# An expert's w1 and v1 products rewritten as seven block products of 64 tokens, two at a time in column halves

## Chip, core and metric

The kernel runs on one core of one Trainium2 chip. The metric is the device time of a launch in microseconds. In the profile PE is TensorE's matmuls, PEld its weight loads, DVE is VectorE, ACT is ScalarE, POOL is GpSimd and SP is the queue that issues most transfers.

## What is computed

Everything is float32. An input of 4 x 1024 tokens with 1024 channels is layer-normed (`xn`), and the result is the sum of three parts:

```
x + attention(xn) + moe(xn)
attention: q = xn Wq, v = xn Wv, a decaying scan of v over the tokens, y = q * state,
           layer norm of y, y * silu(xn Wg), then y Wo
moe:       softmax over 64 experts, the top 8 of each token, at most C = 128 tokens per expert
           h = silu(xg w1') * (xg v1')     xg: 128 tokens x 1024, w1 and v1: 384 x 1024
           out[token] += weight * (h w2)   w2: 384 x 1024
```

The change touches the line `h = ...` for each of the 64 experts.

## The kernel before

**Stages.** The first half of the span, up to about 1225 us, computes v, q and gate for four batch rows. Each 1024 x 1024 product of that half, and the output projection Wo, is already done as a two by two block product with seven instead of eight block products (`steps`, `left_sums`, `right_sums`; the matmuls are line 137). Weight blocks with their sums (tile `w`, seven slots) are read through a pool with two buffers (`pools.left`), one load per product on the SP queue. After that comes the expert stage: a loop over 64 experts, into which 16 units of the output projection (`project`, seven steps of four float32 matmuls each) are spread, so that most experts carry two such steps, some one or three, and the last three none.

**One expert before.** `fetch(e + 2)` loads w1 and v1 two experts ahead and gathers the tokens' rows by an indirect transfer on POOL (line 849). `turned` transposes the gathered rows on DVE (867). `hidden` runs 8 matmuls of 128 tokens x 384 columns for w1 and 8 for v1 (line 884) into two PSUM banks; between the two, PE transposes the hidden values of the expert before (903), which DVE copies to `hT` (904). `gate` is a Silu on ACT (894) and a product on DVE (895). `output` runs six matmuls for w2 (914), scales the rows on DVE (917), and POOL adds them to the output in DRAM (925). A float32 matmul is two records in the profile: 16 matmuls are x32.

**Buffers.** Weights go through five buffers in rotation (`pools.x`, two, and `pools.y`, three), so that three loads per expert can run ahead. PSUM banks come by tag: a, b and c have two buffers each, r and t one.

**Order.** From the fourth expert on, the order on each engine is the scheduler's; only the first three experts are pinned on DVE and PE (`in_order`). A bank or a tile is released by the last instruction that reads it, and a writer waits for that.

Of the kernel before, what the change touches and what calls it, by code (L numbers as in the profile page):

```python
# [8 lines left out]
F32 = mybir.dt.float32  # L9
I32 = mybir.dt.int32  # L10
AF = mybir.ActivationFunctionType
ALU = mybir.AluOpType
# [4 lines left out]
P = 128  # L17
B, S, D = 4, 1024, 1024
NTOK = B * S
KD = D // P  # L20
KH = KD // 2
SH = S // 2
NM = SH // P
E, K, F, C = 64, 8, 384, 128
KF = F // P
Q = 32
NQ = P // Q
DQ = D // NQ
# [12 lines left out]
NSLOT = 7  # L41
# [2 lines left out]
BLOCKS = ((0, 0), (1, 0), (1, 1), (0, 1))  # L44

H0, H1 = slice(0, SH), slice(SH, S)


def left_sums(eng, t, pin=lambda ins: None):

    pin(eng.tensor_tensor(t[:, 4], t[:, 3], t[:, 2], ALU.add))
    eng.tensor_tensor(t[:, 5], t[:, 4], t[:, 0], ALU.subtract)
    eng.tensor_tensor(t[:, 3], t[:, 0], t[:, 3], ALU.subtract)
    eng.tensor_tensor(t[:, 6], t[:, 1], t[:, 5], ALU.subtract)
# [23 lines left out]
@contextmanager  # L78
def in_order(tc, engines=None):

    traced = tc.nc.cur_bb.bb.instructions
    begin = len(traced)
    yield
    last = {}
    for ins in list(traced[begin:]):
        if engines is not None and ins.engine not in engines:
            continue
        if ins.engine in last:
            tc.add_manual_dep(
                ins,  # L90
                last[ins.engine].name,
                mybir.DependencyInfo(mybir.DependencyClass.NoSync, mybir.DependencyReason.DATA),
                reason="in order",
            )
        last[ins.engine] = ins
# [137 lines left out]
def attn_and_routing(  # L233
# [193 lines left out]
    def load_turned(b, h):  # L427
# [5 lines left out]
        for r0, xs, _, _ in stored[b, h]:  # L433
            for j in range(2):
                from_ = rows[r0 + j * P : r0 + (j + 1) * P, :]
                for q in range(NQ):
                    loaded = nc.sync.dma_start(
                        out=xs[q * Q : (q + 1) * Q, j + 1, :].rearrange("i (r c) -> i r c", r=NQ),
                        in_=from_[:, q * DQ : (q + 1) * DQ].rearrange("(r i) c -> i r c", i=Q),
                    )  # L440
# [378 lines left out]
class Experts:  # L819


    def __init__(self, tc, pools, ident, rows, wtab, gated, wo, w1, v1, w2, out):
        self.tc, self.nc, self.pools, self.ident = tc, tc.nc, pools, ident
        self.rows, self.wtab, self.gated = rows, wtab, gated
        self.wo, self.ws, self.out = wo, ((w1, KD), (v1, KD), (w2, KF)), out
        self.weights, self.tokens, self.wo_b, self.loaded = {}, {}, {}, 0

    def load(self, e, n):


        if e >= E:
            return
        pools, (w, k) = self.pools, self.ws[n]
        t = (pools.x if self.loaded % 5 < 2 else pools.y)(f"w{n}_{e}")
        self.loaded += 1
        t = t.rearrange("p a b -> p (a b)")
        self.nc.sync.dma_start(out=t, in_=w[e])
        self.weights[e, n] = t.rearrange("p (k f) -> p k f", k=k)

    def fetch(self, e):  # L840

        if e >= E:
            return
        nc, pools = self.nc, self.pools
        for n in range(2):
            self.load(e, n)
        xg = pools.quarter.tile([P, NQ, DQ], F32, tag="quarter", name=f"xg_{e}")
        for r in range(NQ):
            nc.gpsimd.indirect_dma_start(  # L849
                out=xg[:, r, :],  # L850
                out_offset=None,
                in_=self.rows.rearrange("n (q c) -> (n q) c", q=NQ),
                in_offset=bass.IndirectOffsetOnAxis(ap=self.part[:, r, e : e + 1], axis=0),
            )
        wt = pools.small.tile([P, E], F32, tag="wt", name=f"wt_{e}")
        nc.gpsimd.indirect_dma_start(  # L856
            out=wt,
            out_offset=None,
            in_=self.wtab,
            in_offset=bass.IndirectOffsetOnAxis(ap=self.idx[:, e : e + 1], axis=0),  # L860
        )
        self.tokens[e] = xg, wt[:, e : e + 1]

    def turned(self, e):

        xT = self.pools.line.tile([P, KD, P], F32, tag="line", name=f"xgT_{e}")
        done = self.nc.vector.transpose(  # L867
            xT.rearrange("p k (r i) -> p k r i", i=Q),
            self.tokens[e][0].rearrange("p r (k j) -> p k r j", j=Q),
        )  # L870
        if e == 0:
            self.tc.keep_in_program_order(done)
        return xT

    def hidden(self, e, xT, before):


        pools = self.pools
        ph, hT = [], None
        for n in range(2):  # L880
            ps = pools.bank("ab"[n], [P, F], f"h{n}_{e}")
            w = self.weights.pop((e, n))
            for k in range(KD):
                self.nc.tensor.matmul(  # L884
                    ps, lhsT=xT[:, k, :], rhs=w[:, k, :], start=(k == 0), stop=(k == KD - 1)
                )
            ph.append(ps)
            if n == 0 and before is not None:
                hT = self.turned_hidden(*before)
        return ph, hT  # L890

    def gate(self, e, ph):
        act = self.pools.one.tile([P, F], F32, tag="cur", name=f"act_{e}")
        self.nc.scalar.activation(act, ph[0], AF.Silu)
        self.nc.vector.tensor_tensor(act, act, ph[1], ALU.mult)  # L895
        return act

    def turned_hidden(self, e, act):
        nc, pools = self.nc, self.pools
        hT = pools.line.tile([P, KF, P], F32, tag="line", name=f"hT_{e}")  # L900
        pt = pools.bank("t", [P, KF, P], f"hpt_{e}")
        for j in range(KF):
            nc.tensor.transpose(pt[:, j, :], act[:, j * P : (j + 1) * P], self.ident)  # L903
        nc.vector.tensor_copy(hT, pt)  # L904
        return e, hT

    def output(self, e, hT):
        nc, pools = self.nc, self.pools
        w2, wt = self.weights.pop((e, 2)), self.tokens.pop(e)[1]
        ys = pools.line.tile([P, D], F32, tag="line", name=f"ys_{e}")  # L910
        for h, cols in enumerate((H0, H1)):
            ps = pools.bank("cr"[h], [P, SH], f"y_{e}_{h}")
            for j in range(KF):
                nc.tensor.matmul(  # L914
                    ps, lhsT=hT[:, j, :], rhs=w2[:, j, cols], start=(j == 0), stop=(j == KF - 1)
                )
            nc.vector.tensor_scalar(ys[:, cols], ps, wt, None, ALU.mult)  # L917
            if e == E - 1:
                halves = self.out.rearrange("n (h c) -> (n h) c", h=2)
                self.add(halves, self.ends[:, h : h + 1], ys[:, cols])  # L920
        if e < E - 1:
            self.add(self.out, self.idx[:, e : e + 1], ys)
# [35 lines left out]

    def begin(self, idx, part, ends):
        self.idx, self.part, self.ends = idx, part, ends  # L960
        self.fetch(0)

    def turn_first(self):
        self.turn = self.turned(0)

    def run(self):
        nc, units = self.nc, B * NM
        gated = self.load_gated(0)
        self.fetch(1)
        self.load_wo()  # L970
        self.load(0, 2)


        begins = [1 + u * (E - 4) // units for u in range(units)] + [E - 3]
        before, todo, u, many = None, None, 0, iter(())
        for e in range(E):

            kept = [mybir.EngineType.DVE, mybir.EngineType.PE] if e < 3 else []
            with in_order(self.tc, kept):
                ph, turned_before = self.hidden(e, self.turn, before)  # L980
                self.fetch(e + 2)
                self.load(e + 1, 2)
                if e == 0:
                    self.turn = self.turned(e + 1)
                act = self.gate(e, ph)
                if 0 < e < E - 1:
                    self.turn = self.turned(e + 1)
                if e == 0:
                    right_sums(nc.vector, self.wo_b, lambda n: self.pools.block(f"wo_{n}"))
                if before is not None:  # L990
                    self.output(*turned_before)
                before = e, act
                if u < units and e == begins[u]:
                    todo = self.project(u, gated)
                    many = iter((3, 2, 2) if begins[u + 1] - e == 3 else (2, 2, 2, 1))
                    u += 1
                    gated = self.load_gated(u) if u < units else None
                for _ in range(next(many, 0)):
                    next(todo, None)
        self.output(*self.turned_hidden(*before))  # L1000


# [46 lines left out]
```

## Time and profile before

| | |
|---|---|
| median of 3 runs | 2642.36 us (2641.43 to 2643.7) |
| the profiled execution's own time | 2641.28 us |
| its span | 2639.3 us |
| granted TensorE clock, mean | 0.998 |
| PE busy | 2617.9 us, 99% of the span |
| DVE, ACT, POOL busy | 1108.6, 315.6, 696.5 us |
| DMA in the expert stage (1600 to 2500 us) | 0.86 to 0.91 busy, 274 to 296 GB/s |

Busy times overlap across engines. A group of the profile names the line, the engine, the output and input tiles, the shape and the number of records, then busy time and the mean duration of one. Matmul durations overlap each other[...]; their pace is read from the chain of waits (a start, a length, a count), not from the mean.

### The profile page before, as it was taken

The page shows a single profiled execution, that of the slowest core. Times are in us where ns is not written, and L with a number is a line of the kernel's source. Part 1 is how long each engine was busy: PE and PEld are TensorE (multiplying, and loading weights), DVE is VectorE, ACT ScalarE, POOL GpSimd, SP SyncE. Part 2 cuts the span into 40 slices and gives each one's busy share as a digit, 9 for nine tenths or more (in the row PEclk, how much of TensorE's full clock was granted, in tenths as well). Part 3 has the DMA queues.
Part 4 walks back from the last instruction along what each step waited for, and adds up shares of the span by engine and source line. Part 5 has one row for each costly group of instructions (what it writes and reads, how often), then busy time and mean ns, then how long its engine had stood idle before and what let it go on. Part 6 is the DMA issues. An engine that isn't in the chain of part 4 may idle for free.

```text
span 2639.3 us, 18523 instructions
## 1 busy us (share of the span) xinstructions
PE 2617.9 (99%) x6917; PEld 1269.6 (48%) x6917; DVE 1108.6 (42%) x1414; ACT 315.6 (12%) x472; POOL 696.5 (26%) x631
## 2 busy tenths in 40 slices
PE   9999999999999999999999999999999999999997
PEld 5444444444444444444555555555555555555554
DVE  8946686465935686273222222222222221222221
ACT  4113111131112211121000000000000000000000
POOL 1452312111030102122323323333333333333231
PEclk9999999999999999999999999999999999999999
DMA  5665434442444522328889988899889988999886
GB/s 188 247 199 203 171 127 139 176 171 92 148 131 167 203 84 84 147 97 329 263 269 304 295 287 277 282 296 290 285 280 289 302 280 280 287 288 302 265 282 178
DMA packets 122474, 592.95 MB, mean 225 GB/s; under 512 B 15872, under 2 KB 52736, under 8 KB 89360
## 3 DMA queue, kind: packets, MB, share of 16 engines
q1 hardware_dynamic: 81488, 448.03, 47.4%
q0 software_dynamic: 40464, 143.72, 20.1%
q8 instruction: 55, 0.90, 0.1%
q14 instruction: 35, 0.29, 0.0%
q10 hardware_dynamic: 432, 0.01, 0.0%
HBM read 483.67 MB, written 124.81 MB: 231 GB/s over the span
## 4 chain that ended last, share of the span: by engine, by line
PE 95%; DVE 4%; issue 0%; DMA 0%; POOLq 0%; ACT 0%; DVEq 0%
PE h L884 25%; PE y L914 12%; PE pa_g L137 8%; PE pa_o L137 8%; PE pa_q L137 7%; PE pa_v L137 7%; PE pc_g L137 4%; PE pc_o L137 4%; PE pc_v L137 4%; PE pc_q L137 4%; PE pb_o L137 2%; PE pb_g L137 2%; PE pb_q L137 2%; PE pb_v L137 2%; PE lg L475 1%; DVE cur L548 1%
## 5 line engine op out<-in xcount | busy, mean ns | idle before, releaser
L884 PE MATMUL h<-w,xgT 128*128 128x384 f32 x2048 | 682.1, 486 | 0.0
L884 PEld LDWEIGHTS h<-w,xgT 128*128 128x128 f32 x2048 | 384.5, 190 | 268.9 <-issue 32.5
L849 POOL DMA_INDIRECT xg<-rows,tables x256 | 250.9, 980 | 404.4 <-DVE xgT L867 333.0
L914 PE MATMUL y<-w,hT 128*128 128x512 f32 x768 | 340.1, 592 | 1.0 <-DVE hT L904 1.0
L137 PE MATMUL pa_g<-xT,w 128*128 128x512 f32 x512 | 230.7, 593 | 0.0
L914 PEld LDWEIGHTS y<-w,hT 128*128 128x128 f32 x768 | 145.9, 190 | 170.9 <-issue 153.0
L904 DVE COPY hT<-hpt 128x384 f32<-128x384 f32 x64 | 35.7, 558 | 438.1 <-PE hpt L903 433.4
L137 PE MATMUL pa_q<-xT,w 128*128 128x512 f32 x480 | 216.6, 593 | 3.0 <-DVE y L172 3.0
L137 PE MATMUL pa_v<-xT,w 128*128 128x512 f32 x480 | 215.9, 592 | 0.0
L917 DVE TENSOR_SCALAR ys<-y,wt 128x512 f32<-128x512 f32 x128 | 96.0, 750 | 239.3 <-PE y L914 239.3
L137 PE MATMUL pa_o<-wo_T,gated 128*128 128x512 f32 x384 | 172.6, 592 | 0.0
L137 PEld LDWEIGHTS pa_g<-xT,w 128*128 128x128 f32 x512 | 96.9, 190 | 122.3 <-issue 121.7
L137 PEld LDWEIGHTS pa_v<-xT,w 128*128 128x128 f32 x480 | 91.2, 190 | 114.9 <-issue 109.9
L137 PEld LDWEIGHTS pa_q<-xT,w 128*128 128x128 f32 x480 | 90.5, 190 | 115.9 <-issue 109.7
L925 POOL DMA_INDIRECT out_dram<-ys,tables x63 | 102.2, 1623 | 153.4 <-DMA out_dram<-ohi 105.0
L856 POOL DMA_INDIRECT wt<-wtab,tables x64 | 62.3, 973 | 288.9 <-DVE ys L917 250.5
L684 POOL DMA_DIRECT2D gated<-y x64 | 48.5, 763 | 323.5 <-DVE y L679 312.6
L895 DVE TENSOR_TENSOR act<-act,h 128x384 f32<-128x384 f32 x64 | 35.5, 554 | 229.6 <-PE h L884 229.6
L137 PEld LDWEIGHTS pa_o<-wo_T,gated 128*128 128x128 f32 x384 | 73.0, 190 | 90.9 <-issue 89.9
L137 PE MATMUL pc_g<-xT,w 128*128 128x512 f32 x256 | 115.7, 592 | 0.0
L137 PE MATMUL pc_q<-xT,w 128*128 128x512 f32 x256 | 115.5, 593 | 0.0
L137 PE MATMUL pc_v<-xT,w 128*128 128x512 f32 x256 | 115.4, 593 | 0.0
(210 smaller groups left out, 2474.7 us busy)
## 6 DMA issues: line engine op xcount, KB each, us to landing
w<-in_w_dram SPq DMA_DIRECT2D x128, 1536.0 KB, 7.7
w<-in_v_dram SPq DMA_DIRECT2D x64, 1536.0 KB, 9.7
w<-wsum SPq DMA_DIRECT2D x36, 1792.0 KB, 7.7
wsum<-w POOLq DMA_DIRECT2D x12, 1792.0 KB, 6.1
x<-in_x_dram SPq DMA_DIRECT2D x32, 512.0 KB, 9.2
rows<-x POOLq DMA_DIRECT2D x32, 512.0 KB, 7.4
gated<-y POOLq DMA_DIRECT2D x64, 256.0 KB, 3.3
gated<-gated SPq DMA_DIRECT2D x16, 1024.0 KB, 10.4
```

The lines of the kernel that those rows point to most:

```text
L137: nc.tensor.matmul(ps, lhsT=lhs[:, slot, k, :], rhs=blocks[right][:, k, :], start=start and k == 0, stop=stop and k == KH - 1, skip_group_ ...
L475: nc.tensor.matmul(two[h * E : (h + 1) * E, :], lhsT=r_sb[:, k, :], rhs=blocks[f"B{k // KH + 1}{h + 1}"][:, k % KH, :], start=(k == KD - 1 ...
L548: nc.vector.match_replace(cur, eight, cur, 0.0)
L684: nc.gpsimd.dma_start(out=gated[b, :, :, slot, m, :].rearrange("u p j -> p u j"), in_=yc[:, h * SH : (h + 1) * SH].rearrange("p (u j) -> p ...
L849: nc.gpsimd.indirect_dma_start(out=xg[:, r, :], out_offset=None, in_=self.rows.rearrange("n (q c) -> (n q) c", q=NQ), in_offset=bass.Indir ...
L856: nc.gpsimd.indirect_dma_start(out=wt, out_offset=None, in_=self.wtab, in_offset=bass.IndirectOffsetOnAxis(ap=self.idx[:, e : e + 1], axis=0),
L884: self.nc.tensor.matmul(ps, lhsT=xT[:, k, :], rhs=w[:, k, :], start=(k == 0), stop=(k == KD - 1))
L895: self.nc.vector.tensor_tensor(act, act, ph[1], ALU.mult)
L904: nc.vector.tensor_copy(hT, pt)
L914: nc.tensor.matmul(ps, lhsT=hT[:, j, :], rhs=w2[:, j, cols], start=(j == 0), stop=(j == KF - 1))
L917: nc.vector.tensor_scalar(ys[:, cols], ps, wt, None, ALU.mult)
L925: self.nc.gpsimd.indirect_dma_start(out=to, out_offset=bass.IndirectOffsetOnAxis(ap=rows, axis=0), in_=ys, in_offset=None, compute_op=ALU.add,
```

## The change

The two products of an expert are treated as one product of a two by two block matrix (tokens in halves of 64, channels in halves of 512) with another one (channels in halves of 512, the two blocks of columns being w1 and v1). It takes seven block products of 64 x 512 x 384 instead of eight. A block product has only 64 stationary columns, so two different ones are issued alternately, one to the left and one to the right half of the array's columns (`tile_position`), and land in partitions 0 to 63 and 64 to 127 of a PSUM bank.

DVE forms four sums of the weights (T1 to T4, 128 x 1536 each) and four of the tokens (128 x 256 each) per expert. ACT moves some halves of banks across partitions, DVE adds the products up, and the scaling of the output rows goes from DVE to ACT. PE, DVE and ACT are held in program order through the whole expert stage. w1 and v1 get two fixed buffers each, w2 a single one. One of the two buffers of `pools.left` is now kept for T2 and T3 (`places`), and the first unit of the projection begins with the first expert.

```diff
+ORDERED = [mybir.EngineType.PE, mybir.EngineType.DVE, mybir.EngineType.Activation]
 def load(self, e, n):
-        t = (pools.x if self.loaded % 5 < 2 else pools.y)(f"w{n}_{e}")
+        slot = (n, e % 2) if n < 2 else n
+        if slot not in self.slots:
+            t = (pools.x if e == 0 and n < 2 else pools.y)(f"w{n}_{e}")
+            self.slots[slot] = t.rearrange("p a b -> p (a b)")
+        t = self.slots[slot]
+def places(self):
+        t = pools.left.tile([P, NSLOT, KH, P], F32, tag="w", name="t23")
+        u = pools.block("t4").rearrange("p a b -> p (a b)")
...
+def left_sums(self, e):
+        a11, a12, a21, a22 = self.left_blocks(e)
+        vector.tensor_tensor(s3, a11, a21, ALU.subtract)
+        vector.tensor_tensor(s1, a21, a22, ALU.add)
+        vector.tensor_tensor(s2, s1, a11, ALU.subtract)
+        vector.tensor_tensor(s4, a12, s2, ALU.subtract)
+def sums31(self, e):
+            b11, _, b12, b22 = self.right_blocks(e)
+            self.nc.vector.tensor_tensor(self.t3, b22, b12, ALU.subtract)
+            self.nc.vector.tensor_tensor(b12, b12, b11, ALU.subtract)
+def sums24(self, e):
+            _, b21, t1, b22 = self.right_blocks(e)
+            self.nc.vector.tensor_tensor(self.t2, b22, t1, ALU.subtract)
+            self.nc.vector.tensor_tensor(self.t4, b21, self.t2, ALU.subtract)
 def hidden(self, e):
-        for n in range(2):
-            for k in range(KD):
-                self.nc.tensor.matmul(
-                    ps, lhsT=xT[:, k, :], rhs=w[:, k, :], start=(k == 0), stop=(k == KD - 1)
+        ba, bb, bc, bd = (pools.bank(tag, [P, F], f"h{tag}_{e}") for tag in "abcr")
+        def both(left, right):
+            for k in range(len(left[3])):
+                for half, (bank, a, b, ks) in ((lo, left), (hi, right)):
+                    nc.tensor.matmul(bank[half], lhsT=a[:, ks[k], :], rhs=b[:, ks[k], :],
+                        start=(k == 0), stop=(k == len(ks) - 1), tile_position=(0, half.start))
+        both((bc, s3, self.t3, every), (bc, s4, b22, every))
+        self.sums31(e + 1)
+        both((ba, a11, b11, every), (bb, s1, t1, every))
+        nc.scalar.copy(act[lo], ba[lo])
+        nc.scalar.copy(act[hi], ba[lo])
+        nc.scalar.copy(up[lo], bb[hi])
+        nc.vector.tensor_tensor(mid, bc, act, ALU.add)
+        both((bb, s2, self.t2, every), (bd, a12, b21, every))
+        nc.scalar.copy(up[hi], bb[lo])
+        nc.vector.tensor_tensor(up, mid, up, ALU.add)
+        nc.vector.tensor_tensor(up, bb, up, ALU.add)
+        nc.vector.tensor_tensor(mid[lo], bb[lo], mid[lo], ALU.add)
+        both((bd, a22, self.t4, (0, 1)), (ba, a22, self.t4, (2, 3)))
+        nc.scalar.copy(act[lo], ba[hi])
+        nc.vector.tensor_tensor(act, bd, act, ALU.add)
+        nc.vector.tensor_tensor(act[lo], act[lo], mid[lo], ALU.add)
+        nc.scalar.activation(act, act, AF.Silu)
+        self.turned(e + 1)
+        nc.vector.tensor_tensor(act, act, up, ALU.mult)
+        self.left_sums(e + 1)
+        self.sums24(e + 1)
 def output(self, e):
-            ps = pools.bank("cr"[h], [P, SH], f"y_{e}_{h}")
+            ps = pools.bank("br"[h], [P, SH], f"y_{e}_{h}")
-            nc.vector.tensor_scalar(ys[:, cols], ps, wt, None, ALU.mult)
+            nc.scalar.mul(ys[:, cols], ps, wt)
 def run(self):
-        begins = [1 + u * (E - 4) // units for u in range(units)] + [E - 3]
+        begins = [u and 1 + u * (E - 4) // units for u in range(units)] + [E - 3]
+        with in_order(self.tc, ORDERED):
+            self.sums24(0)
+            for e in range(E):
+                if e > 0:
+                    self.turn_hidden(e - 1)
+                self.hidden(e)
+                self.fetch(e + 2)
+                if e == 0:
+                    right_sums(nc.vector, self.wo_b, lambda n: self.pools.block(f"wo_{n}"))
+                else:
+                    self.output(e - 1)
+                    self.load(e, 2)
...
+            self.turn_hidden(E - 1)
+            self.output(E - 1)
```

The four calls of `both` are called the first to the fourth quarter below; the first three have four pairs of matmuls each, the fourth has two.

More of the change, by code (lines that the diff above doesn't have):

```diff
@@ L25 @@
 KF = F // P
+TH = P // 2
 Q = 32
@@ L825, in __init__ @@
         self.wo, self.ws, self.out = wo, ((w1, KD), (v1, KD), (w2, KF)), out
-        self.weights, self.tokens, self.wo_b, self.loaded = {}, {}, {}, 0
+        self.weights, self.xTs, self.wo_b, self.slots, self.xg = {}, {}, {}, {}, None
     def load(self, e, n):
@@ L833, in load @@
         pools, (w, k) = self.pools, self.ws[n]
-        t = (pools.x if self.loaded % 5 < 2 else pools.y)(f"w{n}_{e}")
-        self.loaded += 1
-        t = t.rearrange("p a b -> p (a b)")
+        slot = (n, e % 2) if n < 2 else n
[3 more added lines that the diff above has]
+        t = self.slots[slot]
         self.nc.sync.dma_start(out=t, in_=w[e])
@@ L844, in fetch @@
         nc, pools = self.nc, self.pools
-        for n in range(2):
+        for n in (1, 0):
             self.load(e, n)
-        xg = pools.quarter.tile([P, NQ, DQ], F32, tag="quarter", name=f"xg_{e}")
+        if self.xg is None:
+            self.xg = pools.block("xg").rearrange("p k (x c) -> p (k x) c", c=DQ)
         for r in range(NQ):
             nc.gpsimd.indirect_dma_start(
-                out=xg[:, r, :],
+                out=self.xg[:, e % 2 * NQ + r, :],
                 out_offset=None,
@@ L854, in fetch @@
             )
-        wt = pools.small.tile([P, E], F32, tag="wt", name=f"wt_{e}")
         nc.gpsimd.indirect_dma_start(
-            out=wt,
+            out=self.wt[:, e % NQ, :],
             out_offset=None,
@@ L861, in fetch @@
         )
-        self.tokens[e] = xg, wt[:, e : e + 1]
+    def places(self):
+        pools = self.pools
+        t = pools.left.tile([P, NSLOT, KH, P], F32, tag="w", name="t23")
+        t = t.rearrange("p a b c -> p (a b c)")
+        u = pools.block("t4").rearrange("p a b -> p (a b)")
+        n = KH * F
+        self.t2, self.t3, self.t4 = (
+            v.rearrange("p (k f) -> p k f", f=F) for v in (t[:, 0:n], t[:, n : 2 * n], u[:, 0:n])
+        )
+        self.up, self.mid = t[:, 2 * n : 2 * n + F], u[:, n : n + F]
+        self.s = pools.one.tile([P, 4, KH, TH], F32, tag="cur", name="s")
     def turned(self, e):
+        if e >= E:
+            return
         xT = self.pools.line.tile([P, KD, P], F32, tag="line", name=f"xgT_{e}")
@@ L868, in turned @@
             xT.rearrange("p k (r i) -> p k r i", i=Q),
-            self.tokens[e][0].rearrange("p r (k j) -> p k r j", j=Q),
+            self.xg[:, e % 2 * NQ : (e % 2 + 1) * NQ].rearrange("p r (k j) -> p k r j", j=Q),
         )
@@ L872, in turned @@
             self.tc.keep_in_program_order(done)
[L873 to L879, printed above, removed]
-        for n in range(2):
-            ps = pools.bank("ab"[n], [P, F], f"h{n}_{e}")
-            w = self.weights.pop((e, n))
-            for k in range(KD):
-                self.nc.tensor.matmul(
-                    ps, lhsT=xT[:, k, :], rhs=w[:, k, :], start=(k == 0), stop=(k == KD - 1)
[L886 to L898, printed above, removed]
-        nc, pools = self.nc, self.pools
[L900 to L905, printed above, removed]
@@ L907, in output @@
-    def output(self, e, hT):
-        nc, pools = self.nc, self.pools
-        w2, wt = self.weights.pop((e, 2)), self.tokens.pop(e)[1]
+        self.xTs[e] = xT
+    def left_sums(self, e):
+        if e >= E:
+            return
+        vector = self.nc.vector
+        a11, a12, a21, a22 = self.left_blocks(e)
+        s1, s2, s3, s4 = (self.s[:, i] for i in range(4))
+        vector.tensor_tensor(s3, a11, a21, ALU.subtract)
+        vector.tensor_tensor(s1, a21, a22, ALU.add)
+        vector.tensor_tensor(s2, s1, a11, ALU.subtract)
+        vector.tensor_tensor(s4, a12, s2, ALU.subtract)
@@ new lines, in left_blocks, with right_blocks @@
+    def left_blocks(self, e):
+        xT = self.xTs[e]
+        return [xT[:, k : k + KH, i : i + TH] for i in (TH, 0) for k in (0, KH)]
+    def right_blocks(self, e):
+        return [self.weights[e, n][:, k : k + KH] for n in range(2) for k in (0, KH)]
+    def sums31(self, e):
+        if e < E:
+            b11, _, b12, b22 = self.right_blocks(e)
+            self.nc.vector.tensor_tensor(self.t3, b22, b12, ALU.subtract)
+            self.nc.vector.tensor_tensor(b12, b12, b11, ALU.subtract)
@@ new lines, in sums24, with hidden @@
+    def sums24(self, e):
+        if e < E:
+            _, b21, t1, b22 = self.right_blocks(e)
+            self.nc.vector.tensor_tensor(self.t2, b22, t1, ALU.subtract)
+            self.nc.vector.tensor_tensor(self.t4, b21, self.t2, ALU.subtract)
+    def hidden(self, e):
+        nc, pools = self.nc, self.pools
+        a11, a12, _, a22 = self.left_blocks(e)
+        b11, b21, t1, b22 = self.right_blocks(e)
+        s1, s2, s3, s4 = (self.s[:, i] for i in range(4))
+        ba, bb, bc, bd = (pools.bank(tag, [P, F], f"h{tag}_{e}") for tag in "abcr")
+        lo, hi = slice(0, TH), slice(TH, P)
+        def both(left, right):
+            for k in range(len(left[3])):
+                for half, (bank, a, b, ks) in ((lo, left), (hi, right)):
+                    nc.tensor.matmul(
+                        bank[half],
+                        lhsT=a[:, ks[k], :],
+                        rhs=b[:, ks[k], :],
+                        start=(k == 0),
+                        stop=(k == len(ks) - 1),
+                        tile_position=(0, half.start),
+                    )
+        every, act, up, mid = range(KH), self.act, self.up, self.mid
+        both((bc, s3, self.t3, every), (bc, s4, b22, every))
[19 more added lines that the diff above has]
+        self.sums24(e + 1)
+        for n in range(2):
+            del self.weights[e, n]
@@ L910, in output, with turn_hidden @@
+    def turn_hidden(self, e):
+        nc, pt = self.nc, self.pools.bank("t", [P, KF, P], f"hpt_{e}")
+        for j in range(KF):
+            nc.tensor.transpose(pt[:, j, :], self.act[:, j * P : (j + 1) * P], self.ident)
+        nc.scalar.copy(self.hT, pt)
+    def output(self, e):
+        nc, pools = self.nc, self.pools
+        w2, wt, hT = self.weights.pop((e, 2)), self.wt[:, e % NQ, e : e + 1], self.hT
         ys = pools.line.tile([P, D], F32, tag="line", name=f"ys_{e}")
         for h, cols in enumerate((H0, H1)):
-            ps = pools.bank("cr"[h], [P, SH], f"y_{e}_{h}")
+            ps = pools.bank("br"[h], [P, SH], f"y_{e}_{h}")
@@ L960, in begin @@
         self.idx, self.part, self.ends = idx, part, ends
+        v = self.pools.line.tile([P, S], F32, tag="line", name="act")
+        self.act, self.hT = v[:, 0:F], v[:, F : 2 * F].rearrange("p (j i) -> p j i", i=P)
+        self.wt = v[:, 2 * F :].rearrange("p (x e) -> p x e", e=E)
         self.fetch(0)
     def turn_first(self):
-        self.turn = self.turned(0)
+        self.places()
+        self.turned(0)
+        self.left_sums(0)
+        self.sums31(0)
     def run(self):
         nc, units = self.nc, B * NM
-        gated = self.load_gated(0)
         self.fetch(1)
         self.load_wo()
+        gated = self.load_gated(0)
         self.load(0, 2)
-        begins = [1 + u * (E - 4) // units for u in range(units)] + [E - 3]
[L975 to L980, printed above, removed]
-                self.fetch(e + 2)
[L982 to L987, printed above, removed]
+        begins = [u and 1 + u * (E - 4) // units for u in range(units)] + [E - 3]
+        todo, u, many = None, 0, iter(())
+        with in_order(self.tc, ORDERED):
[4 more added lines that the diff above has]
+                self.hidden(e)
+                self.fetch(e + 2)
                 if e == 0:
                     right_sums(nc.vector, self.wo_b, lambda n: self.pools.block(f"wo_{n}"))
-                if before is not None:
-                    self.output(*turned_before)
-                before = e, act
+                else:
+                    self.output(e - 1)
+                    self.load(e, 2)
                 if u < units and e == begins[u]:
@@ L996, in run @@
                     u += 1
-                    gated = self.load_gated(u) if u < units else None
                 for _ in range(next(many, 0)):
                     next(todo, None)
-        self.output(*self.turned_hidden(*before))
+                if u < units and e + 1 == begins[u]:
+                    gated = self.load_gated(u)
+            self.turn_hidden(E - 1)
+            self.output(E - 1)
 def kernel(**inputs):
```

## The prediction

> **What bounds the kernel now.** First the page's busy times and its clock row: PE is busy 99% of the span at full clock. Then the costliest groups and the chain that ended last, in order of time:
>
> ```profile
> PE 2617.9 (99%) x6917; PEld 1269.6 (48%) x6917; DVE 1108.6 (42%) x1414; ACT 315.6 (12%) x472; POOL 696.5 (26%) x631
> ...
> PEclk9999999999999999999999999999999999999999
> ```
> ```profile
> 2004.97 5.16 PE h L884 x16
> 2010.13 5.15 PE y L914 x12
> ```
> ```profile
> 908.85 7.09 PE lg L475 x32
> 915.94 1.05 PE pa_g L137 x2
> ...
> 917.43 2.58 PE pc_g L137 x6
> ```
>
> So a stage is worth what it takes from PE, and any wait put into PE's order counts in full. The pace of a record is length over count: 5.16/16 = 0.3225 us for 384 columns, 2.58/6 = 0.430 for 512. An expert's `h` is 32 records, 10.32 us; with the three transposes (0.33) and `y` (5.15) it is 15.8 us, plus 3.43 per step of the output projection.
>
> The rows of the router's logits (L475) are the near relation of the change: 64 stationary columns, the two halves of the array in turn, each with its own moving data. 32 records take 7.09 us, 0.222 each, half of 0.430. The halves run at the same time.
>
> **The change, part by part.**
>
> *Matmuls.* Fourteen pairs of float32 matmuls, 28 pairs of records, replace 32 records: 28 x 0.3225 = 9.03 us, 1.29 less per expert. Here a rule speaks against the change. The Trainium skill, "TensorE: Matmul & The Clock Gate", Part 3, says a weight load overlaps a running matmul only where the two use different rows of the array; both halves use all rows. By the rule each pair would add a load (137 ns in the L475 weight-load group) and cost 0.46, 12.9 us in all, 3.8 more than by the row. The row decides: pairs of 512 ran at the undivided matmul's pace. At 384 columns there is less time for the two loads, but 2 x 137 = 274 ns still lies under 322.
>
> *Switch to halves and back.* The logits' stretch: 7.09 - 16 x 0.430 = 0.21, and the next two whole records take 1.05 instead of 0.86, 0.19 more. I add 0.40 per expert (0.3 to 0.5).
>
> *A wait inside each expert.* In the built program's order the first matmul of the third quarter waits for ScalarE's copy of `bb[hi]` to `up[lo]`, in all 64 experts: that quarter writes the other half of the same bank. In ScalarE's order, now fixed, two other copies stand before it, and all three need the second quarter's end. Nothing follows on PE meanwhile, as the order is fixed. ScalarE's nearest rows:
>
> ```profile
> L894 ACT ACTIVATE act<-h 128x384 f32<-128x384 f32 x64 | 31.4, 490 | 593.5 <-PE hpt L903 590.2 <-PE h L884 3.3
> L299 ACT COPY xT<-pt 128x512 f32<-128x512 f32 x16 | 8.6, 587 | 6.3 <-PE pt L298 6.1
> ```
>
> 384 elements out of PSUM take 490 ns. Sixteen copies of 587 are 8.6 us busy instead of 9.4, in pairs, so neighbours overlap by 0.1: three take 0.39 + 0.39 + 0.49 = 1.27. In the timeline of before `y`'s first record starts at 2009.96 and DVE's L895, which waits for the last of `h`, at 2010.23: a reader starts 0.25 or so after PE has gone on. In the other direction the last `y` follows its `hT` by 0.05 (DVE's copy ends at 2620.30, PE starts at 2620.35). 0.25 + 1.27 + 0.05: 1.57 us of idle PE per expert; ends 1.27 (no latency) and 1.85 (no overlap).
>
> Per expert: -1.29 + 0.40 + 1.57 = +0.68; x 64 = **+43.5 us**. The gain of the seventh-of-eight product is smaller than the wait that serves it.
>
> *A second wait, 13 times.* In the expert after a unit of the projection has begun, `pb_o` still holds a b bank, since DVE adds it up only behind the next weight sums. `y`'s first half then waits for DVE's last read of `hb`: from the third quarter's end 0.25 + copy 0.49 + DVE 0.05 + 0.59 + 0.48 + 0.55 = 2.4, against a fourth quarter of 1.29 and 0.1 of switch: 1.0 each, **+13**. Three units of three experts have their last two steps next to each other, with a DVE sum between: **+3**.
>
> *At the start of the stage: the last gate product.* T2 and T3 take one of the two weight buffers before the last gate product's weights are loaded. Its load now waits for the end of the product before, and PE waits for the load. Two rows, a lone w1 load and a load of this kind:
>
> ```profile
> w<-in_w_dram SPq DMA_DIRECT2D x1, 1536.0 KB, 6.2
> ```
> ```profile
> w<-wsum SPq DMA_DIRECT2D x1, 1792.0 KB, 8.0
> ```
>
> 6.2 x 1792/1536 = 7.2 from issue, 0.6 of latencies, and 0.9 as the last step now follows its DVE read directly: 8.7 (8 to 10). PE is idle for 7.7 of it. The Trainium skill, same page, Part 1, says the clock falls to half after an idle window of about 3.4 us. No run of before has such an idle in its middle, but its start shows the price:
>
> ```profile
> 2.08 7.81 PE L246 MATMUL warm<-zero,ident 128*128 128x512 f32 x12 [2.08 <-DVE best L273]
> ```
>
> Twelve records of 0.43 would be 5.15, and the last one's tail 0.16: 2.5 lost. By the row alone a gap in the middle could cost nothing; by the rule each gap over 3.4 costs 2.5, while 1.57 costs none. I take the rule: **+11.2**.
>
> *Expert 1.* Behind the weight sums for expert 1, DVE has the four sums of Wo (4 x 2.32 from L64's 2291 ns) and four of the projection's left block (2.6). By a clock from the start of `hidden(0)`: quarters end at 2.8 and 5.4, after the wait at 9.5 and 10.8. DVE's `mid[lo]` ends 2.4 after the third, at 11.9; two more adds (554 ns each) bring 13.0, the transpose (1234) 14.2, the product 14.7, four token sums 16.3, T2 and T4 19.8. Then 9.3 for Wo and 2.6: 31.8; then 3.5 of sums for expert 2, which in program order come before expert 1's own `mid`; four combinations later, near 37.5, `mid[lo]` is done. PE had two projection steps (6.9), the transposes (0.3) and `hidden(1)` (10.9) behind 10.9, so at 29.0 it needs the bank: 8.5 idle, 7.5 beyond the 1.0 counted, and the clock 2.5: **+10** (5 to 12).
>
> *The end.* w2 has one buffer. Expert 63's load is issued after `y` of 62 and needed at once: 6.2 to 8.3, say 6.7, + 0.3, less the 1.5 that PE waits for `hT` there anyway: 5.5, and the clock 2.5: **+8** (5 to 10).
>
> *At nothing.* DVE's four weight sums are 1.76 each (2291 x 1536/2048, + 40 ns), the token sums 1.7, with the combinations, the transpose and a share of the projection 15 us per expert of some 22.5; on the clock of expert 0 above, s3 and s4 are ready at 16.3, and PE asks for them at 16.4 even without a projection step (10.9 + 5.15 + 0.33), at 20 to 23 with one or two. If DVE were later by x in each expert, x would come on top, 64-fold. The next expert's weights are now needed at 3 us into `hidden`, some 20 us earlier than before; their loads are issued from 5.4 and 9.5 us on in the expert before, so 14 to 20 us remain for a landing of 7.7 to 9.8 (page, part 6). Scaling on ScalarE (0.6 twice) leaves it under 6 us busy per expert. POOL's list is the same; its index transfers overlap DVE's two-input sums in before without either growing (683 ns with and without).
>
> Sum: 43.5 + 13 + 3 + 11.2 + 10 + 8 = 88.7 on the profiled execution's 2641.28, which stands 1.1 under the median: **2730 us**, 3.3% slower.
>
> **Rivals.**
> - *The wait inside each expert is not paid.* If copies of half a bank's partitions took far less than 490 ns, or PE got the bank at once, an expert would gain 1.29 - 0.40 = 0.89, 57 us in all, against at most 32 of start, end and unit stalls left (the 13 shrink with it): 2641 - 57 + 32 = 2616, faster. It decides from a wait under 0.2 us on. Against it: the copies cannot begin before the second quarter ends, and 490 ns is a measured row for as many elements. Chance 0.05.
> - *The halves don't run together at 384 columns*, by the skill's rule: 64 x 3.8 = +246, 2975. Against it the L475 rows. Chance 0.04.
> - *DVE or the transfers are late in every expert*: 15 us of chained DVE work with some 1 to 2 us of slack at `y`'s second half, or weights that land after they are asked for. One us per expert is +64: 2795. For it: the DMA engines are at 0.9 already, in order DVE stalls as a whole; against: the stage gets slower, so transfers get more time. Chance 0.13.
> - *The forecast*: 0.78. Its own range: the wait 1.27 to 1.85 is -19 to +18, start and end -12 to +7, the switch 6 either way; not all together, so 2700 to 2758.
>
> **Numbers.** 2730 for the likeliest. The range reaches to 2697 below, and to 2790 above, for part of the late-DVE case; left out are the faster case, the separate halves and the rest of that. Faster by over 0.2% (what a measurement of this kernel can tell from no change) 0.05, within it 0.02, slower 0.93.
>
> **What would show it.** PE idle some 1.6 us before the third quarter in each expert, put down to ScalarE's copy; matmul pairs 0.32 apart; PE busy time down by 60 to 80 us, its idle time up by over 100; a gap of 7 to 8 us before the last gate product, one near 8 in expert 1, one of 5 to 7 before the last `y`, with the granted clock down behind them. It is wrong if the third quarter starts on time, or if PE waits for DVE's sums or for weights in steady state.

## The result, and the profile after

The changed kernel takes 2738.57 us (median of 4 runs, 2737.7 to 2738.86), the kernel before, beside it, 2641.89 (4 runs). The ratio is 1.0364, 95% interval 1.0346 to 1.0382: 3.6% slower. The profiled execution took 2738.45 us with a span of 2736.6, 97.2 more than the profiled execution of before.

From the page of the changed kernel, the two rows that answer to those of before (PE 2617.9 us, 99%):

```profile
PE 2581.3 (94%) x8453; PEld 1129.0 (41%) x8453; DVE 1712.3 (63%) x2118; ACT 584.1 (21%) x984; POOL 856.5 (31%) x631
...
PEclk9999999999999999999999999999999999999998
```

PE is busy for 37 us less and idle for 134 us more. What ended that idle time stands in PE's waits (what waited, for whom: us in total, times, the longest):

```profile
PE hb L942 <- ACT t L957: 97.7, 64, 1.5
PE y L989 <- DVE t L963: 19.3, 13, 7.8
PE pa_g L139 <- DMA w<-wsum: 8.6, 1, 8.6
PE y L989 <- DMA w<-in_w_dram: 7.3, 1, 7.3
```

Beside these, PE in the expert stage waits only 2.4 us in three places, for DVE between neighbouring projection steps. The first row is the wait in each expert; the chain of waits (start, us, what) shows how it is made, in an expert with two projection steps:

```profile
1300.47 0.06 PE hb L942
1300.53 0.04 ACT act L955
1300.57 0.43 issue
1300.99 0.48 ACT act L956
1301.47 0.01 issue
1301.49 0.48 ACT t L957
1301.97 0.04 issue
1302.01 0.54 PE hb L942
...
1306.11 5.35 PE y L989 x12
```

L955, L956 and L957 are ScalarE's three copies. They run one behind the other, their starts 0.48 to 0.50 us apart, and the third quarter's first matmul (`hb`, 1302.01) follows the last of them by 0.04. By the starts of PE's records, a matmul that should follow 0.322 us after the last one follows 2.02 us after it, in 63 of the 64 experts (1.40 in expert 0): 1.70 us of wait.

The single gaps, in the same view: the last gate product (5.21 us for eight records that otherwise take 3.43), expert 1, and the end.

```profile
1208.41 8.57 DMA w<-wsum
1216.98 0.04 issue
1217.02 5.21 PE pa_g L139 x8
1222.23 3.43 PE pb_g L139 x8
```
```profile
1280.23 7.74 PE y L989 x12
```
```profile
2711.21 7.49 DMA w<-in_w_dram
2718.70 0.14 issue
2718.84 4.37 PE y L989 x6
```

Each is followed by matmuls at half pace: 7.74 us where the rows of other experts have 5.35. The granted clock behind the first gap is 0.50 from 1217.0 to 1219.0 us, and 1.00 from 1222.3 on.

### The profile page after: what moved, and what is told of

It reads as the page before. It is cut to its first block, busy times and chain, and to the rows that moved or that the text cites. A ratio compares the mean times of both kernels' runs of the same rounds, so it can differ in the third digit from the quotient of the medians.

```text
span 2736.6 us, 23206 instructions
## 1 busy us (share of the span) xinstructions
PE 2581.3 (94%) x8453; PEld 1129.0 (41%) x8453; DVE 1712.3 (63%) x2118; ACT 584.1 (21%) x984; POOL 856.5 (31%) x631
## 4 chain that ended last, share of the span: by engine, by line
PE 89%; DVE 5%; ACT 3%; issue 2%; DMA 1%; POOLq 0%; SPq 0%; DVEq 0%
PE y L989 13%; PE pa_g L139 8%; PE pa_o L139 8%; PE pa_q L139 7%; PE hb L942 7%; PE pa_v L139 7%; PE hc L942 6%; PE ha L942 6%; PE pc_g L139 4%; PE pc_o L139 4%; PE pc_v L139 4%; PE pc_q L139 4%; PE hr L942 2%; PE pb_g L139 2%; PE pb_o L139 2%; PE pb_q L139 2%
## 5 line engine op out<-in xcount | busy, mean ns | idle before, releaser
L854 POOL DMA_INDIRECT xg<-rows,tables x256 | 395.3, 1544 | 620.8 <-DVE xgT L886 558.7
L989 PE MATMUL y<-w,act 128*128 128x512 f32 x768 | 350.5, 606 | 26.6 <-DVE t L963 19.3
L919 DVE TENSOR_TENSOR t<-w 128x1536 f32<-128x1536 f32 x64 | 112.5, 1757 | 259.9 <-PE hc L942 259.9
L942 PE MATMUL hb<-t,s 128*64 128x384 f32 x512 | 178.8, 492 | 97.7 <-ACT t L957 97.7
L989 PEld LDWEIGHTS y<-w,act 128*128 128x128 f32 x768 | 142.2, 192 | 220.8 <-issue 167.3
L942 PE MATMUL hc<-t,s 128*64 128x384 f32 x512 | 179.1, 492 | 0.0
L942 PE MATMUL hc<-w,s 128*64 128x384 f32 x512 | 179.1, 492 | 0.0
L942 PE MATMUL hr<-w,xgT 128*64 128x384 f32 x512 | 178.8, 492 | 0.0
L942 PE MATMUL ha<-w,xgT 128*64 128x384 f32 x512 | 175.6, 486 | 0.0
L942 PE MATMUL hb<-w,s 128*64 128x384 f32 x512 | 175.6, 486 | 0.0
```

Source lines behind the costliest of these rows:

```text
L854: nc.gpsimd.indirect_dma_start(out=self.xg[:, e % 2 * NQ + r, :], out_offset=None, in_=self.rows.rearrange("n (q c) -> (n q) c", q=NQ), in ...
L919: self.nc.vector.tensor_tensor(self.t3, b22, b12, ALU.subtract)
L942: nc.tensor.matmul(bank[half], lhsT=a[:, ks[k], :], rhs=b[:, ks[k], :], start=(k == 0), stop=(k == len(ks) - 1), tile_position=(0, half.st ...
L989: nc.tensor.matmul(ps, lhsT=hT[:, j, :], rhs=w2[:, j, cols], start=(j == 0), stop=(j == KF - 1))
```

## The experiments

Times are medians; "before" is the kernel before, run beside each group of experiments: 2641.93 us for 1 to 4, 2642.26 for 5 to 8, 2642.44 for 9 and 10. The edits are shown in part; `...` stands for lines left out.

**1. Halves alone.** The kernel before, with each `h` matmul issued as two of 64 tokens in the two column halves.

```diff
-                self.nc.tensor.matmul(
-                    ps, lhsT=xT[:, k, :], rhs=w[:, k, :], start=(k == 0), stop=(k == KD - 1)
-                )
+                for i in (0, P // 2):
+                    self.nc.tensor.matmul(ps[i : i + P // 2], lhsT=xT[:, k, i : i + P // 2],
+                        rhs=w[:, k, :], start=(k == 0), stop=(k == KD - 1), tile_position=(0, i))
```

> The kernel before, with each of its sixteen h matmuls per expert issued as two of 64 tokens, one in each half of the array's columns; still eight block products' worth of work, no sums, no copies. It measures the pace of a pair and the price of going to halves and back by themselves. My theory: a pair of 384 columns takes 0.3225 us like the undivided matmul, and each stretch of halves costs 0.35 to 0.40 on the way in and out; there are two stretches per expert here, since the three transposes stand between w1 and v1: 64 x 2 x 0.35 to 0.40 = +45 to +51, so 2687 to 2693 us. Rival one: the switch costs nothing inside an expert (what I read from the logits rows was something else): 2642. Rival two: the halves don't overlap and a pair costs twice a record: +10.3 x 64 = 3300.

Measured: 2687.35 us, ratio 1.0173 (1.0156 to 1.019), +45.4. Its chain of waits, for the transposes, the product of v1 and `y`:

```profile
2007.26 0.48 PE hpt L909 x3
2007.74 5.31 PE h L885 x32
2013.05 5.35 PE y L920 x12
```

32 records in 16 pairs take 5.31 us; 16 undivided ones took 5.16. The pairs keep the pace of 0.322, and what comes on top stands at the edges: 0.15 going in, 0.15 to 0.20 on the first whole matmuls behind (`hpt` 0.48 instead of 0.33, `y` 5.35 instead of 5.15). By the starts of the transposes an expert with two projection steps takes 23.31 us instead of 22.67, 0.32 per stretch. My theory held; both rivals fell.

**2. The order of ScalarE's copies.** One line moved.

```diff
+        nc.scalar.copy(up[lo], bb[hi])
         nc.scalar.copy(act[lo], ba[lo])
         nc.scalar.copy(act[hi], ba[lo])
-        nc.scalar.copy(up[lo], bb[hi])
```

> The changed kernel with one line moved: ScalarE copies bb[hi] to up[lo], the copy that the third quarter waits for, before the two copies into act instead of behind them. My theory (the wait is a start-up of about 0.25 and three copies of 0.48 one behind the other, 1.70 measured): two copies leave the wait, 0.75 is left, 63 x 0.95 = -60, so 2679 us. Rival: the third quarter needs all of ScalarE's copies or DVE's sums at that moment, or PE is held by something else that only ends at the same time: 2738, no change.

Measured: 2679.18 us, ratio to before 1.0141 (1.0124 to 1.0158), 59 us less than the changed kernel. PE's waits:

```profile
PE hb L942 <- ACT t L955: 36.8, 64, 0.6
```

The wait now names the first copy and falls from 97.7 to 36.8. So it is the read of `bb`'s other half that holds the third quarter, plus whatever stands ahead of it in ScalarE's order. That the quarter waits for a read of the other half is set in the built program; whether it has to was not tried.

**3. The order of the quarters.** The quarter that fills `ba` and `bb` goes first, so that the copies run under the `bc` quarter.

```diff
-        both((bc, s3, self.t3, every), (bc, s4, b22, every))
-        self.sums31(e + 1)
         both((ba, a11, b11, every), (bb, s1, t1, every))
         nc.scalar.copy(act[lo], ba[lo])
         nc.scalar.copy(act[hi], ba[lo])
         nc.scalar.copy(up[lo], bb[hi])
+        both((bc, s3, self.t3, every), (bc, s4, b22, every))
+        self.sums31(e + 1)
         nc.vector.tensor_tensor(mid, bc, act, ALU.add)
```

> The changed kernel with the second quarter (ba, bb) issued before the first (bc), so that ScalarE's three copies run while PE computes bc. My theory: the 1.70 us before the third quarter go in 63 experts, -107; DVE's combinations now start later (the weight sums for the next expert wait for the bc quarter), so y's first half waits longer in the 13 experts after a unit has begun, +6 to +20: 2637 to 2652 us, and what stays over before's time is the start, the end and expert 1. Rival: the wait only moves, because DVE has some 15 us of chained work in each expert and now gets its first operand 2.6 us later, so PE waits for DVE before the transposes or y: +1 to +2 us per expert, 2700 to 2760.

Measured: 2648.15 us, ratio 1.0024 (1.0013 to 1.0034): the change's loss is down to 6 us by moving two lines. PE's waits:

```profile
PE y L989 <- DVE t L963: 33.8, 13, 9.9
```

This is now the first row; that of `hb` is gone. The wait of `y` for DVE's L963 has grown by 14.5 us, within the +6 to +20 expected. An expert with two steps takes 21.72 us, 0.95 less than before: 1.29 from the block product less 0.34, which is what is left for the halves (experiment 1 measured 0.32 per stretch by itself). The block product does pay on PE; its wait ate it.

**4. The start and the end.** The last gate product takes its weight buffer before T2 and T3 take theirs, and the last w2 goes into a buffer that is free by then.

```diff
-        slot = (n, e % 2) if n < 2 else n
+        slot = (n, e % 2) if n < 2 else (0, e % 2 ^ 1) if e == E - 1 else n
...
+            w = weights(b, 2, m)
             if m == NM - 1 and b == B - 1:
                 turn_first()
-            left = gates(m, left)
+            left = gates(m, left, w)
```

> The changed kernel with two edits: the last gate product's weights take their buffer before T2 and T3 take theirs, and the last expert's w2 goes into the buffer that w1 of expert 62 has left, so that it is loaded a whole expert earlier. My theory: the gap of 9.2 us before the last gate product and of 7.6 us before the last y go, and with them the slow matmuls behind each (1.8 us each): -8.6 - 1.8 - 6.3 - 1.8 = -18.5, so 2720 us. Rival: the sums into T3 now wait for the end of the product before the last, and DVE holds up the last gate product's own work behind them, so the start's part comes back as a wait before expert 0: 2730.

Measured: 2719.66 us, ratio 1.0294 (1.0276 to 1.0311), 18.9 less than the changed kernel. Both rows of transfers are gone from PE's waits, and no wait before expert 0 has come in their place.

**5. The bank of y's first half.** On top of the swapped quarters, `y` goes to the banks it had before the change.

```diff
-            ps = pools.bank("br"[h], [P, SH], f"y_{e}_{h}")
+            ps = pools.bank("cr"[h], [P, SH], f"y_{e}_{h}")
```

> The version with the quarters swapped, with y's first half back in a c bank, as before the change, instead of a b bank. A c bank of the expert is only read by the first combination on DVE, some 1.5 us ahead of the last read of hb. My theory: the 12 waits of 2 us before y's first half (33.8 us with the one of expert 1) shrink to some 0.3 us in the experts over which the projection holds its own c bank, and expert 1 keeps 8.4 of 9.9: 2648 - 21 = 2627 us. Rival: what holds y there is DVE as a whole and not that bank, so the same time comes back before y's second half or before the transposes: 2645 to 2650.

Measured: 2626.4 us, ratio 0.9936 (0.9919 to 0.9952). PE's waits:

```profile
PE y L989 <- DVE act L966: 7.6, 1, 7.6
...
PE y L989 <- DVE t L958: 3.7, 16, 0.2
```

The 33.8 us for L963 have become 3.7 for the first combination, L958, in 16 experts, and 7.6 in expert 1. It was the bank.

**6. These edits together (3, 4 and 5).**

> Quarters swapped, y's first half in a c bank, and the two edits at the start and the end. If the parts add up: 2627 - 18.5 = 2608 us, 1.3% faster than the kernel before. Rival: the parts share a limit (DVE, or the transfers at 0.9 busy, which now have 1.7 us less for each expert), and the sum falls short by 10 us or more: 2618 to 2640.

Measured: 2607.32 us, ratio 0.9866 (0.985 to 0.9883). The parts add up to within 1 us.

**7. Wo's sums in two parts.** Two of the four sums in expert 0, two in expert 1, and the first unit's steps as 2, 1, 2, 2.

```diff
-                    right_sums(nc.vector, self.wo_b, lambda n: self.pools.block(f"wo_{n}"))
+                    wo_sums = right_sums_parted(nc.vector, self.wo_b, lambda n: self.pools.block(f"wo_{n}"))
+                    next(wo_sums)
...
+                if e == 1:
+                    next(wo_sums)
```

> As all_four, and the four sums of Wo on DVE in two parts, two in expert 0 and two in expert 1, with the first unit's seven steps spread as 2, 1, 2, 2 over the experts. My theory: the wait of expert 1 falls by two sums, 4.6 us, and the slow matmuls behind it (2.8 us) go: 2601 us. Rival: DVE stays behind through experts 1 to 3, and the wait moves to expert 2: 2608.

Measured: 2602.87 us, ratio 0.9851 (0.9835 to 0.9868). Expert 1's wait falls from 7.6 to 2.9 us, by the 4.6 of two sums. The matmuls behind it still run at half pace for a while, so 4.5 us came and not 7.

**8. One more sum on DVE, ahead of the combinations.** T3 is formed twice in each expert; what is computed stays the same.

```diff
             self.nc.vector.tensor_tensor(self.t3, b22, b12, ALU.subtract)
+            self.nc.vector.tensor_tensor(self.t3, b22, b12, ALU.subtract)
```

> As all_four_wo_parted, with one weight sum (T3, 128 x 1536, 1.76 us on DVE) done twice in every expert, so that DVE has 1.76 us more of work ahead of the combinations. It asks what DVE's idle time is worth; with the quarters swapped DVE is 64% busy, and in an expert with two projection steps it waits 5.7 us for PE. My theory: in that version the last read of hr (the first add into act) ends 0.2 us before y's second half needs its bank, so the order eats the idle time up: 1.76 - 0.2 = 1.55 late in every expert, 64 x 1.55 = +99, so 2700 us. Rival: the idle time of DVE takes the sum in, except in the last three experts: +0 to +5, 2601 to 2606.

Measured: 2726.98 us, ratio 1.0323 (1.0306 to 1.0341), +124 on experiment 7. PE's waits:

```profile
PE y L1007 <- DVE act L984: 70.1, 46, 6.8
PE y L1007 <- DVE t L976: 32.4, 16, 2.0
```

L984 is the first add into `act`, which frees the bank of `y`'s second half: late by 1.59 us in 44 experts, as expected. In 16 others the first half is late by 2.2 instead (2.51 from start to start), and behind nine of these the clock falls for a while; expert 1 waits 6.8 us instead of 2.9. These make most of the 27 us above the expected 2700. DVE was 67% busy.

**9. The same sum behind the combinations.** T2 is formed twice instead of T3.

```diff
             self.nc.vector.tensor_tensor(self.t2, b22, t1, ALU.subtract)
+            self.nc.vector.tensor_tensor(self.t2, b22, t1, ALU.subtract)
```

> As all_four_wo_parted, with the extra sum of 1.76 us on DVE at another place than in one_more_sum: T2 is formed twice, behind the combinations, just ahead of the idle time in which DVE waits for the bc quarter of the next expert. My theory: what counts is the place in the order; here DVE has 5.7 us of idle time in an expert with two projection steps, 2.3 in one with one, and only the last three experts, with none, are late, by about 1.2 each: 2603 + 0 to 5 = 2603 to 2608 us, against 2727 for the same sum ahead of the combinations. Rival: it is the amount of DVE work (67% busy) or its use of the memory beside the transfers that costs, wherever it is put: near 2727.

Measured: 2617.78 us, ratio 0.9906 (0.9891 to 0.9921), +15 on experiment 7. PE's waits:

```profile
PE pa_o L155 <- DVE ohi L190: 10.0, 3, 3.3
PE y L1007 <- DVE act L984: 4.7, 1, 4.7
```

DVE is busier still (69%), at an eighth of the price. Most experts take the sum in. I expected 0 to 5, from the last three experts, and was wrong twice: those take no longer than in experiment 7, and I had left out the places where DVE was behind already. By the starts of the transposes, experts 1 and 3 take 3.2 and 3.5 us longer, and the three units with neighbouring last steps 10 us together.

**10. The first combination ahead of the weight sums.** On experiment 7:

```diff
+        nc.vector.tensor_tensor(mid, bc, act, ALU.add)
         self.sums31(e + 1)
-        nc.vector.tensor_tensor(mid, bc, act, ALU.add)
```

> As all_four_wo_parted, with DVE's first combination (mid, which reads bc) ahead of the two weight sums for the next expert instead of behind them. My theory: y's first half, which waits 0.24 us for mid in 16 experts, no longer does, -3.8, and nothing else moves, since the weight sums end before the third quarter's copies anyway: 2599 us. Rival: the two weight sums, 0.6 us later, push the other combinations and y's second half late: 2603 to 2640.

Measured: 2597.44 us (5 runs), ratio 0.9827 (0.9814 to 0.984). The row of 16 waits for L975 is gone, and those experts take 21.72 us instead of 22.03, 5 us in all. My theory held. This is the fastest version: 1.7% under the kernel before, 5.2% under the change as it was made, with the same seven block products. Its page:

```profile
PE 2562.7 (99%) x8453; PEld 1133.2 (44%) x8453; DVE 1699.8 (65%) x2118; ACT 584.6 (23%) x984; POOL 862.3 (33%) x631
```

## Why the prediction was right, and where its terms were off

The prediction said 2730 and the waits came where it named them; 8.6 us are missing, nearly all of them in the wait inside each expert. So it was not luck: the other terms are each within 1 us, but for the switch. One sign failed, though, and one reading was wrong; both are told below.

- **Matmuls.** 28 pair slots at 0.322 us: right, in the changed kernel (the records of a pair start 0.01 apart, the pairs 0.32) and by itself in experiment 1. The Trainium skill's rule ("TensorE: Matmul & The Clock Gate", Part 3), that a weight load overlaps a matmul only on different rows of the array, would have given +246 us; two column halves over all rows ran together here too. The row of the logits was the right guide.
- **Switch.** Put at 0.40; 0.34 in experiment 3, 0.32 per stretch in experiment 1: 4 us too much over 64 experts, which hid a part of the next term's miss.
- **Wait in each expert.** The largest term, and the one that was too small: 1.57 foretold, 1.70 measured from start to start. The working took ScalarE's neighbours to overlap by 0.1, which it read off the busy time of another group (8.6 us against 16 x 0.587). Three copies here follow each other at 0.48 to 0.50, 1.46 from the first start to the last end instead of 1.27; why these don't overlap is open. Per expert the sum became +0.81 (23.48 against 22.67 us, median of 43 experts) instead of +0.68: 51.8 us instead of 43.5. -1.29 + 0.34 + 1.70 is 0.75 of it. Of the 0.06 left, 0.05 stands at the first pair behind the wait: the next one follows it by 0.37 instead of 0.32, as behind the first pair of a stretch.
- **y's first half.** 13 x 1.0 foretold; 12 waits of 1.03 (1.446 us from start to start, against 0.416 in the other experts), 12.4, and expert 1. Experiment 5 shows, with the quarters swapped, that the bank was the cause.
- **Adjacent steps.** 3 x 1.0 foretold; 1.38 instead of 0.43 from start to start, 3 x 0.95.
- **Last gate product.** 11.2 foretold. Measured: 8.8 of gap (9.24 from start to start instead of 0.43), 0.95 for the step before, 1.8 for slow matmuls, 11.5.
- **Expert 1.** 10 + 1 foretold: 7.8 of gap and 2.4 of slow matmuls, 10.2. **The end.** 8 foretold: 7.60 instead of 1.25 from the transposes to `y`, and 1.8, 8.2. Experiment 4 took start and end away together: 18.9 against 11.5 + 8.2 = 19.7.
- **At nothing.** Right for PE's waits: none in steady state for weights or for DVE's weight and token sums. But POOL's index transfers, said not to grow, did. The 683 ns are DVE's sums; the gathers beside the projection's sums took 947 to 1467 ns in the kernel before, against 955 (median) with DVE idle. That is hidden on PE (last section).
- **PE's busy time.** The sign was 60 to 80 us less; it fell by 37. Matmuls and switch are 64 x (1.29 - 0.34) = 61. The slow matmuls take 6 of it back, and 11 are the end of the record ahead of each wait, which counts as busy (64 x 1.70 = 109, where the row of waits has 97.7). The rest is not traced. The time does not hang on this.

Measured terms: 51.8 + 12.4 + 2.8 + 11.5 + 10.2 + 8.2 = 96.9, against 97.2 between the two executions. It closes better than it should: the attention stage of this execution also lost some 2.7 us (one step of q came 1.0 later, and slow matmuls followed), which other runs with the same code there show only in part, so the sum is good to about 4 us.

The rival that was faster than before, the wait not paid, needed copies of half the partitions to take far less than 490 ns, or PE to get the bank at once. The wait of 1.70 refutes the second, the groups of the changed kernel (busy us, mean ns, idle before) the first: 64 partitions take what 128 take.

```profile
L980 ACT COPY act<-hpt 128x384 f32<-128x384 f32 x64 | 30.8, 481 | 135.4 <-PE hpt L979 135.4
L957 ACT COPY t<-hb 64x384 f32<-64x384 f32 x64 | 30.4, 475 | 1.6
```

The rival of a late DVE did not happen in this order of the quarters, but experiments 3 and 8 show how near it is: with the quarters swapped, 1.76 us more ahead of the combinations cost 124 us.

## What to carry to other kernels

A saving on the engine that bounds the kernel is not safe until the readers of its results are placed: here 1.29 us of PE per expert were saved, 0.34 went to the halves and 1.70 to a wait, because the next product wrote into a bank whose other half was still to be read, and ScalarE had two other copies queued first. When such a wait is found, reorder independent products so that the readers run under one of them, before giving the idea up. And an engine's idle share is no slack (DVE was 67% busy when one more sum cost 124 us): count what stands in its order between the wait's end and the instruction that frees the next bank.

## What the runs showed of the hardware

**The clock and the length of a gap.** Counted from the last gate product on, in the ten traces with the seven block products, by the starts of PE's records: of 231 gaps of 1.0 to 1.9 us, the waits of 1.70 among them, one was followed within 8 us by matmuls at half pace (0.85 us a record instead of 0.43). Of 33 gaps of 2.1 to 2.9 us it was 12, of 6 gaps of 3.1 to 3.5 us 5, and of 16 gaps of 4.9 us and more, all. The Trainium skill ("TensorE: Matmul & The Clock Gate", Part 1) puts the window at about 3.4 us; here the share of falls rises between 1.9 and 2.2. Length is not all that counts: of the 33, the 16 in experiment 8 were followed by nine falls and the 17 in the other traces by three, at much the same lengths. What else decides is open. A fall cost 1.8 to 2.4 us in the changed kernel, so the 2.5 that the prediction took lay just above them.

**Index transfers under DVE's sums.** POOL's gathers of token rows take 1544 ns each in the changed kernel. In the kernel before it was 980, and in experiment 1, which has the halves but not the sums, 973. The group in the changed kernel:

```profile
L854 POOL DMA_INDIRECT xg<-rows,tables x256 | 395.3, 1544 | 620.8 <-DVE xgT L886 558.7
```

With one more sum on DVE it is 1590 (experiment 8) and 1647 (experiment 9). The changed kernel's trace tells why the mean grew, in the four gathers of one expert (start, us):

```profile
2003.95 1.67 POOL L854 DMA_INDIRECT xg<-rows,tables  x1 [10.81 <-DVE xgT L886]
2005.93 2.27 POOL L854 DMA_INDIRECT xg<-rows,tables  x1 [0.30 <-issue]
2008.50 1.56 POOL L854 DMA_INDIRECT xg<-rows,tables  x1 [0.30 <-issue]
2010.36 0.94 POOL L854 DMA_INDIRECT xg<-rows,tables  x1 [0.30 <-issue]
```

DVE forms the token sums and T2 and T4 from 2004.05 to 2009.24, and the first three gathers fall into that time. Over the whole trace, the 46 gathers during which DVE does nothing take 946 ns (median), and the 61 that meet both T2 and T4 take 2269. DVE's sums take the same either way (T3 1758 ns with an index transfer beside it and without). So the gathers grow beside these sums, which have both inputs in SBUF. Whether that is what counts is not settled: beside L895, which reads one input from PSUM, 68 gathers of the kernel before take 946 ns (median), but the two overlap for only 240. What DVE and POOL share was not tried. PE waits for none of it here.
